# A message-passing kernel whose row gathers wait on the vector engine: the waits of the first 18 groups are taken out, and the distance cutoff becomes one activation

## The chip, the cores and the metric

The kernel runs on one core of a Trainium2 chip. The metric is the time of one execution in device microseconds (us). A core has several engines that run side by side and wait for each other through semaphores: TensorE (PE; its weight loads are listed as PEld), VectorE (DVE), ScalarE (ACT), GpSimd (POOL) and SyncE (SP). SP, ACT and POOL also issue DMA transfers; a name with q behind it (SPq, ACTq, POOLq) is the queue of such an engine.

## The reference, cut to what matters

There are N = 12500 nodes with 64 features (`x`) and E = 200000 edges with 64 features; the edges are sorted by their destination `dst`.

```python
nodes = x[[src, dst]].reshape(E, 128)
gates = ssp(edge_attr @ We1 + be1) @ We2 + be2
soft_cutoff = 1.0 - sigmoid(5.0 * (edge_weight1 - (CUTOFF - 1.5)))    # CUTOFF = 5
h = ssp(nodes @ Wn1 + bn1) @ Wn2 + bn2
message_sum = zeros.at[dst].add(h * gates * soft_cutoff)
new = x + ssp(message_sum @ Ws1 + bs1) @ Ws2 + bs2
out = layernorm(x + new)                     # ssp(v) = softplus(v) - log(2)
```

## The kernel before, in words

**Groups.** The edges are cut into 391 groups of 512; a group is four columns of 128 edges, one edge to a partition. The source rows `x[src]` of a group come by four gathers on POOL's queue (`gather`, line 230): an indirect DMA takes 128 row numbers from `src_i` and puts 128 rows of 64 floats into the tile `xg`. POOL does nothing else but these gathers; there are 1523 of them. In 40 places from group 28 on a column's 128 rows are instead copied row by row by plain DMAs of SP and ACT (`fetch`, line 250); the padding at the end needs none.

**Buffers.** `xg` has AHEAD + BEHIND = 14 + 4 = 18 buffers. Groups 0 to 17 find a fresh one; group g from 18 on waits for the matmul that reads group g - 18's buffer last (`scatter`, line 371).

**Before the loop.** SP loads `src_i`, the destinations, the transposed `x` (in seven parts, line 493), the distances (`cut`) and more. From these the kernel works out the offsets of each half group's window of destinations, and it makes a table of x @ Wn1's lower half in memory: seven parts of two halves (lines 576 to 586), each half by matmuls (L581), two copies out of PSUM, one by ACT (L583) and one by DVE (L584), a store (L585) and a DVE memset that clears the space for the sums (L586). In the third part (`i == 2`, lines 598 to 606) the cutoff is worked out in place in `cut`: DVE's `tensor_scalar` (L599), ACT's sigmoid (L600), which needs a table load before it and one behind it (L601), and DVE's second `tensor_scalar` (L602). DVE goes on with the cast of `rel` (L603) and two subtractions (L606).

**When a gather may start.** Groups 0 to 4 (FREE = 5) wait only for `src_i`. Groups 5 to 13 stand in `waiting`: they are handed out over the halves of the table (lines 587 and 588). Groups 14 to 17 are asked for in steps 0 to 3 of the loop (line 641, `i < BEHIND`). For both, `gather(g, after=True)` first has DVE write one column of the new tile (line 223), so POOL's gather waits until DVE has come to that instruction in its own order.

**The loop.** Step i (lines 632 and on) is an order written out by hand. SP loads for group i + 5, POOL gets group i + 14's gathers, PE runs layer 1 of group i + 1, layer 2 of the group before it and `scatter` of group i - 3; PE also transposes group i + 3 (L299), which is where a gather's data is first read. All of a step's waits are put on its first matmul, `layer1_bias` (L309): it waits for loads of group i + 1 and for the gathers of group i + 3. From step 380 on the distances are shorter. 25 blocks of nodes are finished in between as soon as their edges are complete. The tail behind the last group takes the last block.

Of the kernel before, what the change touches and what calls it, by code (L numbers as in the profile page):

```python
# [42 lines left out]
F32 = mybir.dt.float32  # L43
# [3 lines left out]
AF = mybir.ActivationFunctionType  # L47
OP = mybir.AluOpType
# [9 lines left out]
P = 128  # L58
# [8 lines left out]
AHEAD = 14  # L67
# [1 line left out]
SPREADS = 5  # L69
CATCH_UP = 10  # L70
PREPARE = 5
FREE = 5
BEHIND = 4


# [4 lines left out]
CUTOFF = 5.0  # L80
# [41 lines left out]
def gnn_resnorm_kernel(ctx: ExitStack, tc: tile.TileContext, a: dict, out: bass.AP, E: int):  # L122
    nc = tc.nc
# [42 lines left out]
    packed, at = {}, 0  # L166
# [48 lines left out]
    def padding(g, k):  # L215
        return g * GE + k % 2 * HE + k // 2 * P >= E

    def gather(g, after=False):

        xg = loads.tile([P, K, P], F32, name="xg", bufs=AHEAD + BEHIND)  # L220
        xgs[g] = xg
        if after:
            nc.vector.memset(xg[:, 0, :1], 0.0)
        for k in range(K):
            if (g, k) in by_rows:
                continue
            if padding(g, k):
                nc.vector.memset(xg[:, k, :D], 0.0)
                continue
            note(("gather", g), nc.gpsimd.indirect_dma_start(  # L230
                out=xg[:, k, :D], out_offset=None, in_=x,
                in_offset=bass.IndirectOffsetOnAxis(ap=src_i[:, g, k : k + 1], axis=0)))
# [124 lines left out]
    def layer2(g):  # L357
        layer2_edge(g)
        layer2_node(g)
# [118 lines left out]
    with tc.manual_schedule():  # L478
# [4 lines left out]
        with tc.tile_pool(name="prep", bufs=1) as prep:  # L483
# [3 lines left out]
            PARTS = 7  # L487
# [10 lines left out]
            dist = cut.rearrange("p g k -> p (g k)")  # L498
# [1 line left out]
            dst_i = rel.bitcast(I32)  # L500
            nc.sync.dma_start(dst_i.rearrange("p g k -> p (g k)"), a["dst_l"])

            waiting = {}
            for g in range(AHEAD):
                if g < FREE:
                    gather(g)
                else:
                    waiting.setdefault(min(5 * (g - FREE) // 3, 2 * PARTS - 1), []).append(g)

            nc.vector.memset(one, 1.0)  # L510
            nc.vector.memset(half, 0.5)
# [1 line left out]
            nc.vector.memset(ones3, 1.0)  # L513
            nln2 = prep.tile([P, 1], F32, name="nln2")
            nc.vector.memset(nln2, -LN2)
            brow = prep.tile([1, 4, D], F32, name="brow")
            nc.scalar.dma_start(brow.rearrange("o i d -> o (i d)"), a["biases"])
            nc.scalar.dma_start(consts[:, FIRST:], a["consts"][:, FIRST:])
# [57 lines left out]
            for i in range(PARTS):  # L576
                for c in range(i * CP, (i + 1) * CP, CP // 2):
                    m = CP // 2
                    ps = z_tile().rearrange("p b (k f) -> p (b k) f", k=K)
                    for k in range(m):  # L580
                        nc.tensor.matmul(ps[:, k, :], xT[:, c + k, :], wnb, start=True, stop=True)  # L581
                    tb = prep.tile([P, m, 2 * D], F32, name="tb", bufs=6)
                    nc.scalar.copy(tb[:, :K, :], ps[:, :K, :])  # L583
                    nc.vector.tensor_copy(tb[:, K:, :], ps[:, K:m, :])  # L584
                    nc.sync.dma_start(by_node[:, c : c + m], tb)  # L585
                    nc.vector.memset(sums[:, c * P : WIDE if c + m == NCH else (c + m) * P], 0.0)  # L586
                    for g in waiting.get(c // m, []):
                        gather(g, after=True)
                if i == 1:
                    nc.vector.tensor_copy(base_i[:1], base_b[:1])  # L590
                    nc.vector.tensor_scalar(base_i[32:33], base_b[32:33], float(8 * D), None, OP.mult)
                    nc.vector.tensor_scalar(rows_i, rows_i, float(4 * D), None, OP.mult)
                    for k in range(2):
                        nc.vector.tensor_copy(be3[:, k, :], rows[:, 0, :])
                    for k in range(K):
                        nc.vector.tensor_copy(row3[:, :, k, :], rows[:, 1:3, :])
                        nc.vector.tensor_copy(rs3[:, k, :], rows[:, 3, :])
                if i == 2:
                    nc.vector.tensor_scalar(dist, dist, CUTOFF - 1.5, 5.0, OP.subtract, OP.mult)  # L599
                    nc.scalar.activation(dist, dist, AF.Sigmoid)  # L600
                    nc.scalar.preload_act_table_set("natural_log_exp_and_others")  # L601
                    nc.vector.tensor_scalar(dist, dist, -1.0, 1.0, OP.mult, OP.add)  # L602
                    nc.vector.tensor_copy(rel, dst_i)  # L603
                    for t in range(2):
                        r = rel[:, :, 2 * t : 2 * t + 2]
                        nc.vector.tensor_sub(r, r, base_b[:, :NH].rearrange("p (g h) -> p g h", h=2))  # L606


        with tc.tile_pool(name="finish", bufs=1) as finish:
# [16 lines left out]
            def at(f, g, *more):  # L626
                if 0 <= g < NG:
                    f(g, *more)
# [5 lines left out]
            for i in range(-3, last - 1):  # L634
                now = parts.pop(i, [])
                early = [part for part in now if part.tensor]
                at(load, i + LOADS)
                fetch(i, 0, 0)
                fetch(i, 0, 1)
                if i >= 0:  # L640
                    at(gather, i + AHEAD, i < BEHIND)
                if i < ends:
                    needs = [("xcopy", i + 1), ("load", i + 1)]
                    needs += [(name, g) for g in ahead[i] for name in ("gather", "onehot")]
                    if i >= -1:
                        layer1_bias(i + 1, *needs)
                    for g in second[i]:
                        layer2_edge(g)
                    if i >= -1:
                        layer1_edge(i + 1)  # L650
                        for part in early:
                            part.tensor(tx_tile())
                    if i >= -1:
                        layer1_node(i + 1)
                    for n, g in enumerate(third[i]):
                        scatter(g, zs[i + 1][:, 1, HE + 2 * W * n : HE + 2 * W * (n + 1)])
                    at(exps, i + 1)
                    fetch(i, 1, 0, 0, ROWS // 2)
                    at(logs, i + 1)
                    fetch(i, 1, 0, ROWS // 2, ROWS // 2)  # L660
                    for g in ahead[i]:
                        transposes(g)
                        xcopy(g)
                    fetch(i, 1, 1)
                    for g in second[i]:
                        layer2_node(g)
                    for g in second[i]:
                        hcut(g)
                        message(g)
                    for g in third[i]:  # L670
                        window(g)
                    for part in early:
                        part.others()
                    at(softplus, i + 1)
                else:
                    for g in ahead[i]:
                        transposes(g)
                        xcopy(g)
                    layer1_bias(i + 1)
                    layer1_edge(i + 1)  # L680
                    for part in early:
                        part.tensor(zs[i + 1][:, 1, HE:])
                    layer1_node(i + 1)
                    exps(i + 1)
                    logs(i + 1)
                    for g in second[i]:
                        layer2(g)
                        hcut(g)
                        message(g)
                    softplus(i + 1)  # L690
                    for g in third[i]:
                        scatter(g, tx_tile()[:, : 2 * W])
                        window(g)
                    for part in early:
                        part.others()
                for g in ahead[i]:
                    at(onehot, g + 2)
                for part in now:
                    if not part.tensor:
                        part.others()  # L700
                complete = third[i][-1] + 1 if third[i] else 0
                if blocks and complete >= blocks[0][1] - PREPARE and not begun:
                    begun = node_block(*blocks[0][0], finish)
                    begun.pop(0).others()
                if blocks and complete >= blocks[0][1]:
                    steps = next(steps for steps in BLOCK_STEPS if i + steps[-1] < last - 1)
                    for n, part in zip(steps, begun):
                        parts.setdefault(i + n, []).append(part)
                    rest = begun[len(steps) :]
                    blocks.pop(0)  # L710
                    begun = None
# [12 lines left out]
            square, variance, root, scale, store = (part.others for part in rest)  # L724
# [31 lines left out]
    with tc.If(far > 0), tc.tile_pool(name="outside", bufs=1) as o:  # L756
# [7 lines left out]
        with tc.For_i(0, NG, 1) as g:  # L764
# [13 lines left out]
            xg = o.tile([P, K, 2, D], F32, name="xg2")  # L778
# [120 lines left out]
```

## Time and profile before

| | us |
|---|---|
| three runs, lowest / median / highest | 1963.82 / 1969.16 / 1975.15 |
| the profiled execution, own time | 1968.45 |
| its span in the trace | 1966.5 |
| PE busy in the span | 1750.5 (89%) |
| POOL busy | 1445.0 (73%) |
| DVE busy | 1077.2 (55%) |
| ACT busy | 922.5 (47%) |
| first gather starts / last gather starts | 3.2 / 1919.7 |
| first matmul of layer 1 (L309) | 78.2 |

The busy time of an engine leaves out register moves, semaphore instructions and the issue of DMAs. A line of the timeline has a start, a duration, the engine, the line of the kernel, the operation, what it writes and reads, and in square brackets the idle time just before it with what ended it. In the table of stretches each engine has its busy time and, in parentheses, the number of its instructions.

### The profile page before, as it was taken

Reading aid. Unit: us, or ns where it says so; the run is one execution under the profiler, and the core shown is the slowest. Engines: PE = TensorE matmul, PEld = TensorE weight load, DVE = VectorE, ACT = ScalarE, POOL = GpSimd, SP = SyncE. Lnnn points to the kernel's source line nnn. Section 1 sums busy time; section 2 is a strip of 40 time slices with the busy share of each in tenths; the row PEclk is TensorE's granted clock in tenths of the full one; section 3 lists DMA queues with packets and bytes.
Section 4 is the critical chain, followed back from the end, with each engine's and each line's share of the span. In section 5 each row is a group of like instructions: output and inputs, shape, how many; then the busy total and the mean of one; then the engine's idle time right before and its main releaser. Section 6 shows DMA issues by size and latency. Waiting matters only on the chain.

```text
span 1966.5 us, 46634 instructions
## 1 busy us (share of the span) xinstructions
PE 1750.5 (89%) x11373; PEld 1491.4 (76%) x11373; DVE 1077.2 (55%) x2774; ACT 922.5 (47%) x1318; POOL 1445.0 (73%) x1527
## 2 busy tenths in 40 slices
PE   5899999999998988889889988998989989998896
PEld 4777877877777777777777777777777777777775
DVE  4455555555555555555555555555555555555654
ACT  1344545555454444445444444444544454444443
POOL 6777777777777777777777777777777777777770
PEclk9999999999999999999999999999999999999997
DMA  8422222222222222222222222222222222222220
GB/s 242 128 70 65 70 64 72 65 72 65 73 67 73 65 73 67 67 66 69 65 69 66 67 70 67 69 67 70 68 70 73 64 74 68 70 72 71 69 61 13
DMA packets 149240, 143.45 MB, mean 73 GB/s; under 512 B 50073, under 2 KB 96621, under 8 KB 148964
## 3 DMA queue, kind: packets, MB, share of 16 engines
q1 hardware_dynamic: 92972, 88.12, 15.6%
q0 software_dynamic: 48736, 50.00, 11.3%
q10 hardware_dynamic: 7256, 2.27, 0.6%
q8 instruction: 97, 1.59, 0.3%
q14 instruction: 179, 1.47, 0.3%
HBM read 130.59 MB, written 9.63 MB: 71 GB/s over the span
## 4 chain that ended last, share of the span: by engine, by line
PE 46%; ACTq 14%; DMA 10%; SPq 10%; issue 9%; ACT 5%; DVE 3%; POOL 3%; DVEq 0%; POOLq 0%
ACTq L250 11%; PE z L320 10%; PE gh L348 7%; PE gh L354 6%; PE z L314 5%; PE z L371 5%; DMA xg<-in_x,src_i 4%; PE tx L299 4%; DMA wns<-table 4%; SPq L250 4%; ACT u L331 3%; ACTq L244 3%; PE z L309 3%; POOL xg L230 3%; PE gh L345 2%
## 5 line engine op out<-in xcount | busy, mean ns | idle before, releaser
L230 POOL DMA_INDIRECT xg<-in_x,src_i x1523 | 1444.8, 949 | 475.3 <-issue 319.4
L331 ACT ACTIVATE u<-z 128x768 f32<-128x768 f32 x392 | 315.9, 806 | 624.4 <-PE z L371 316.7
L334 ACT ACTIVATE u<-u,one 128x768 f32<-128x768 f32 x392 | 366.0, 934 | 238.5 <-ACT u L331 236.7
L339 DVE SCALAR_TENSOR_TENSOR s<-u,z 128x768 f32<-128x768 f32 x392 | 372.6, 950 | 171.2 <-ACT u L334 154.6
L363 DVE TENSOR_TENSOR h<-gh,cut 128x256 f32<-128x256 f32 x391 | 165.2, 423 | 478.3 <-PE gh L354 472.0
L320 PE MATMUL z<-xT,wns 106*128 106x256 f32 x1564 | 423.9, 395 | 0.0
L354 PE MATMUL gh<-consts,s 128*128 128x64 f32 x3128 | 395.7, 270 | 0.0
L354 PEld LDWEIGHTS gh<-consts,s 128*128 128x128 f32 x3128 | 384.7, 194 | 0.0
L320 PEld LDWEIGHTS z<-xT,wns 106*128 106x128 f32 x1564 | 307.4, 198 | 45.8 <-ACT xT L304 0.7
L348 PEld LDWEIGHTS gh<-consts,s 128*128 128x128 f32 x1564 | 206.7, 192 | 122.8 <-issue 122.3
L348 PE MATMUL gh<-consts,s 128*128 128x128 f32 x1564 | 282.4, 304 | 0.0
L371 PEld LDWEIGHTS z<-xg,msg 128*128 128x128 f32 x1512 | 237.9, 199 | 22.9
L309 PE MATMUL z<-ones,be 3*128 3x256 bf16 x391 | 105.3, 269 | 167.8 <-DMA wns<-table 64.9
L299 PE MATMUL tx<-consts,xg 128*106 128x128 f32 x1524 | 240.8, 280 | 4.0 <-DVE xg L285 2.7
L388 DVE TENSOR_TENSOR sums<-sums,z 64x42 f32 x756 | 148.7, 197 | 171.4 <-ACT u L331 75.2
L314 PE MATMUL z<-eT,consts 128*128 128x256 f32 x782 | 242.4, 393 | 0.0
L304 ACT COPY xT<-tx 106x512 f32<-106x512 f32 x391 | 221.6, 567 | 15.5 <-PE tx L299 15.3
L371 PE MATMUL z<-xg,msg 128*128 128x84 f32 x1512 | 223.3, 271 | 0.0
L309 PEld LDWEIGHTS <-be 3*128 3x128 bf16 x391 | 35.4, 91 | 206.6 <-issue 102.9
L299 PEld LDWEIGHTS tx<-consts,xg 128*106 128x106 f32 x1524 | 181.8, 144 | 5.1 <-DVE xg L285 3.0
L367 DVE TENSOR_TENSOR msg<-gh,h 128x256 f32<-128x256 f32 x391 | 165.9, 424 | 13.4
L345 PE MATMUL gh<-row,ones 3*128 3x512 bf16 x391 | 145.9, 373 | 0.0
(103 smaller groups left out, 714.0 us busy)
## 6 DMA issues: line engine op xcount, KB each, us to landing
eT<-in_eT SPq DMA_DIRECT2D x195, 256.0 KB
xr<-in_x ACTq DMA_DIRECT2D x2944, 0.2 KB
xr<-in_x SPq DMA_DIRECT2D x2176, 0.2 KB
xg<-in_x,src_i POOLq DMA_INDIRECT x1523
wns<-table SPq DMA_DIRECT2D x782, 21.0 KB
table<-tb SPq DMA_DIRECT2D x14, 448.0 KB
sums<-in_xT SPq DMA_DIRECT2D x7, 455.0 KB
y<-in_x SPq DMA_DIRECT2D x24, 128.0 KB
```

The source lines that it names most:

```text
L230: note(("gather", g), nc.gpsimd.indirect_dma_start(out=xg[:, k, :D], out_offset=None, in_=x, in_offset=bass.IndirectOffsetOnAxis(ap=src_i[ ...
L250: ins = queues[queue].dma_start(row_tiles[n, "in"][r + j : r + j + 1, :D].bitcast(U8), x_bytes[:, bass.ds(row_at[queue][j], 4 * D)])
L299: nc.tensor.transpose(tx[:, k, :], xgs[g][:, k, :DW], ident)
L304: note(("xcopy", g), nc.scalar.copy(xT, xTs[g]))
L314: nc.tensor.matmul(zs[g][:, 0, :HE], we1.rearrange("a h d -> a (h d)"), eTs[g], start=False, stop=True, skip_group_check=True)
L320: nc.tensor.matmul(zn, wns[:, g % REST, h, :], xTs[g][:, h], start=True, stop=True, skip_group_check=True)
L331: nc.scalar.activation(us[g][:, part], z_of(g)[:, part], AF.Exp)
L334: nc.scalar.activation(us[g][:, part], us[g][:, part], AF.Ln, bias=one)
L339: nc.vector.scalar_tensor_tensor(ss[g].rearrange("p i t e -> p (i t e)")[:, part], us[g][:, part], BIG, z_of(g)[:, part], OP.min, OP.max)
L348: nc.tensor.matmul(v[:, 0, t], ss[g][:, 0, t, :], we2, start=False, stop=False, skip_group_check=True)
L354: nc.tensor.matmul(ghs[g][:, 1, 2 * t + h, :], ss[g][:, 1 + h, t, :], wn2, start=False, stop=h == 1 and t == 1, skip_group_check=True)
L371: ins = nc.tensor.matmul(sc, msgs[g][:, 2 * t : 2 * t + 2, :].rearrange("p h f -> p (h f)"), xgs[g][:, 2 * t : 2 * t + 2, D:DW], start=t = ...
```

## The change

It takes the parameter `after` out of `gather`, with its memset on DVE, and the lists `waiting` and `FREE`. All 14 groups that are issued before the loop are issued at one place ahead of the table, and groups 14 to 17 in steps 0 to 3 as before; none of them writes to its tile on DVE first. The cutoff 1 - sigmoid(5 (d - 3.5)) is computed as sigmoid(-5 d + 17.5), with the scale as a number and the bias in a new column `steep`; the two `tensor_scalar` operations on DVE go.

```diff
-FREE = 5
...
-    def gather(g, after=False):
+    def gather(g):
         xg = loads.tile([P, K, P], F32, name="xg", bufs=AHEAD + BEHIND)
         xgs[g] = xg
-        if after:
-            nc.vector.memset(xg[:, 0, :1], 0.0)
...
-            waiting = {}
             for g in range(AHEAD):
-                if g < FREE:
-                    gather(g)
-                else:
-                    waiting.setdefault(min(5 * (g - FREE) // 3, 2 * PARTS - 1), []).append(g)
+                gather(g)
...
+            steep = prep.tile([P, 1], F32, name="steep")
+            nc.vector.memset(steep, 5.0 * (CUTOFF - 1.5))
...
-                    for g in waiting.get(c // m, []):
-                        gather(g, after=True)
...
                 if i == 2:
-                    nc.vector.tensor_scalar(dist, dist, CUTOFF - 1.5, 5.0, OP.subtract, OP.mult)
-                    nc.scalar.activation(dist, dist, AF.Sigmoid)
+                    nc.scalar.activation(dist, dist, AF.Sigmoid, bias=steep, scale=-5.0)
                     nc.scalar.preload_act_table_set("natural_log_exp_and_others")
-                    nc.vector.tensor_scalar(dist, dist, -1.0, 1.0, OP.mult, OP.add)
...
                 if i >= 0:
-                    at(gather, i + AHEAD, i < BEHIND)
+                    at(gather, i + AHEAD)
```

## The prediction

> **What bounds the kernel now.** I read the list of costliest groups first. PE is the busiest engine, but POOL's line catches the eye:
>
> ```profile
> L230 POOL DMA_INDIRECT xg<-in_x,src_i x1523 | 1444.8, 949 | 475.3 <-issue 319.4
> ```
>
> Busy plus idle is 1444.8 + 475.3 = 1920 us: POOL issues gathers from start to end, and the idle time is the same 0.30 us before each. The table of stretches shows whether it ever pauses (POOL is the fifth engine):
>
> ```profile
> 100.00:484.00 384.00, 357.00 (x2425) 305.63 (x2423) 209.18 (x539) 192.89 (x264) 290.33 (x308) 1.00 0.27 68
> 484.00:1885.00 1401.00, 1261.48 (x8259) 1075.55 (x8259) 780.56 (x2008) 673.41 (x969) 1059.68 (x1120) 0.97 0.27 69
> ```
>
> 384 / 308 = 1.247 and 1401 / 1120 = 1.251 us per gather, in the free early part and in the late one alike. So POOL is a clock that ticks every 1.249 us (0.944 + 0.305) and waits for no buffer. Is PE tied to it? The early steps take about 4.35 us on PE, four gathers take 5.0 us, so the 11 groups of lead that the gathers have at 85 us are used up: by the counts of instructions up to 480 us, 92 steps have begun and only one gather is to spare. From there they go together. Up to 1497 us the trace has 301 first matmuls and 1185 gathers; the next step needs groups up to 303, which are 304 x 4 - 31 columns taken by rows = 1185 gathers: exactly the last one issued. At fourteen sampled times from 600 to 1850 us the last gather needed lies within 3 of the last one issued. The waits at L309 name other transfers too (`wns`, 64.9 us); but at 1497 us SP has issued 614 of them, 307 groups, six ahead of need, so the gather in the same wait explains them better. The last touch is late:
>
> ```profile
> 1857.03 0.94 POOL L230 DMA_INDIRECT xg<-in_x,src_i  x1 [0.30 <-DVE l_s L422]
> ...
> 1859.54 0.26 PE L309 MATMUL z<-ones,be 3*128 3x256 bf16 x1 [0.61 <-DMA xg<-in_x,src_i]
> ```
>
> The matmul starts 2.5 us after the gather that it needs. Behind this PE runs on its own to the end, 107 us. So the time is the gathers' stream up to here plus a constant, and **whatever moves the stream moves the end.** Where does POOL lose time? Its own timeline has two holes:
>
> ```profile
> 27.83 0.94 POOL L230 DMA_INDIRECT xg<-in_x,src_i  x1 [0.30 <-issue]
> 33.07 0.94 POOL L230 DMA_INDIRECT xg<-in_x,src_i  x1 [4.30 <-DVE xg L223]
> ...
> 79.19 0.94 POOL L230 DMA_INDIRECT xg<-in_x,src_i  x1 [0.30 <-issue]
> 84.75 0.94 POOL L230 DMA_INDIRECT xg<-in_x,src_i  x1 [4.61 <-DVE xg L223]
> ```
>
> Both end with DVE's memset: group 5 waits for the table's first half, group 14 for step 0.
>
> **The change part by part.** *The holes.* Start to start they are 5.24 and 5.56 us instead of 1.249: 3.99 + 4.31 = 8.3 us. With no wait on DVE both go. The other 11 memsets of this kind held nothing: POOL came to them later than DVE.
>
> *What is late next.* Group 18 is the first to need a used buffer, that of group 0. POOL would reach it at 3.21 + 72 x 1.249 + 2.3 (stretches, below) = 95.4 us. Group 0's scatter in the old trace:
>
> ```profile
> 94.83 0.57 PE L371 MATMUL z<-xg,msg 128*128 128x84 f32 x4
> ```
>
> It ends at 95.40, so even an unmoved start of the loop costs POOL about 0.1 us. Later groups are no danger: scatters follow every 4.35 us, gathers every 5.0.
>
> *The stretches.* Some gathers take longer beside certain DVE operations:
>
> ```profile
> 45.82 1.58 POOL L230 DMA_INDIRECT xg<-in_x,src_i  x1 [0.30 <-issue]
> 46.31 0.97 DVE L599 TENSOR_SCALAR cut<-cut 128x1564 f32<-128x1564 f32 x1
> ...
> 47.31 1.51 ACT L600 ACTIVATE cut<-cut 128x1564 f32<-128x1564 f32 x1 [1.16 <-DVE cut L599]
> ...
> 48.83 1.28 ACT L601 ACT_TABLE_LOAD   x1
> 48.85 0.97 DVE L602 TENSOR_SCALAR cut<-cut 128x1564 f32<-128x1564 f32 x1 [1.57 <-ACT cut L600]
> 48.95 1.88 POOL L230 DMA_INDIRECT xg<-in_x,src_i  x1 [0.30 <-issue]
> 49.74 0.97 DVE L603 CAST rel<-rel 128x1564 f32<-128x1564 int32 x1
> ```
>
> Against 0.944 us the gather at 45.82 loses 0.63 beside L599, that at 48.95 loses 0.93 beside L602 and L603, and one at 51.13 (1.40 us) loses 0.45 beside L606: 2.0 in all. L599 and L602 go. L603 and L606 stay and now follow each other without a pause; by these rows they cost between 0 and 2.0, and I take the middle of L603's 0 to 0.97, 0.5, and L606's 0.45. Saved: 2.0 - 0.95 = 1.0 us, bounds 0 and 2.0. The other stretches before group 18 (0.55 beside the cast L523, 0.27 beside L590, some of 0.1) stay; with the 0.95 they are the 2.3 used above. The Trainium skill, "SBUF — State Buffer", section "Who interferes with whom", says that copy, cast and tensor_scalar can take the port pair that DVE shares with GpSimd and then block it for the whole instruction, while tensor_tensor is not seen to stall descriptor generation. The row beside L606, a tensor_tensor, speaks against the second half. By the page alone only the cast would remain, and the estimate would be 0.4 us more saved.
>
> *The cutoff.* In the old trace ACT waits 1.16 us for L599 and its two table copies for DVE's chain; the table's PE work stands still until 53.12. Without the pair the sigmoid can start when its table is loaded, 46.15, and ends at 47.66; the second load (1.28) lets ACT copy at 48.96, not 50.13. DVE does L603 and L606 from 46.4 to 49.2 and can copy at 49.6, not 52.52. The table and the loop start 2.9 us earlier. Scale and bias on the activation: the nearest rows are Exp without a bias column (0.806 us) and Ln with one (0.934), so at most 0.13 us more; the new memset is 0.06 us in DVE's wait for `dst_h` (8.64 us). Both are hidden. The 2.9 us are worth **nothing at the end**, since PE has 11 groups of lead to use up before it meets the gathers; they only keep group 18's wait at zero. If PE were the bound, they would be the whole gain.
>
> *The transfers brought forward.* 52 gathers (groups 5 to 17) start up to 9 us earlier, in a stretch where the DMA engines are 65% to 87% busy. Their queue took 11.3% of 1966.5 us for 1523 gathers, 0.146 us of all engines each. At most 9.3 / 1.249 = 7 more gathers lie in the stretch ahead of the loop: 1.1 us, below the 2.9 saved; nothing on SP or ACT is moved. The Trainium skill, "DMA: Bandwidth & Descriptors", section "Issuing engines are not separate DMA queues", speaks against the change: DMAs of all engines interleave on the same 16 engines, so a gather issued early takes its turn from the table's stores. By the estimate of the row above, this leaves the sum as it is; the page gives no price for it.
>
> **Sum.** 8.3 + 1.0 = 9.3 us off the stream, and off the profiled execution's 1968.45: **1959.2 us**. The trace's span would be 1957.2. The median of the runs lies 0.7 above the profiled execution; against it 1959.2 is 0.51% faster, against its own time 0.47%. Can PE follow? It must win 9.3 us between its first meeting with the gathers at 480 us and the last at 1859. Its waits at L309 that name a gather sum to 21.2 us, with those that name `wns` 86 us. It can.
>
> **The rivals.**
> - *PE, not POOL, becomes the bound.* If the `wns` waits are real, SP paces many steps. For: SP's queue is nearly without pause in the middle. Against: it waits for PE's scatters 5 to 9 us in every 100 us there, so it has room. If PE gets only the earlier start of 2.9 us and some of the 21.2 us, the gain is 3 to 6 us: 1962.5 to 1965.5.
> - *The gathers still wait.* Group 5 or 14 could be held by something that the memset hid, a buffer or the second part of `src_i`. Against: all 18 buffers are fresh, and that load was issued at 1.22 us, ahead of `dst_h`, which was there at 9.85. Then only the stretches are gained: 1967.5.
> - *Slower: crowded DMA delays the table, and group 18's wait eats the gain.* Until 29 us, where gathers run without a gap, two small dependent transfers took 8.05 (`low_d`) and 6.77 us (`base_b`); around 75 us, behind fewer gathers, the table's last store took 2.81 and the first `wns` 1.89. If five dependent transfers ahead of the loop (a part of `x`, two of the eight halves that reuse a buffer of `tb` and so wait for an earlier store, the last store, `wns`) each rise by 5.5 us, scatter(0) comes 27.5 - 2.9 = 24.6 us later and POOL stands still as long: 24.6 - 9.3 = 15.3 us slower, 1983.8. It decides from a loop start that is 9.3 us later than now; from 19 us later the loss passes 0.5%. Against it: 1.1 us of engine time, as above.
>
> **Chances.** Forecast 0.70 (bounds 1958.2 to 1960.2; the three runs before differ by 0.3% either way, so a median may fall 4 us to a side); PE bound 0.14; gathers still wait 0.08; slower 0.08. The range leaves out the slow case and a little below: from 1958.2 less 0.3%, 1952, to 1970. Faster by over 0.5%, about what a measurement of this kernel can tell from no change, means below 1959.3: the forecast lies on the line, and two thirds of it, 0.47, I put below, since the stretches could save a little more. Within 0.5%: the rest of the forecast, the PE bound and the waiting gathers, 0.23 + 0.14 + 0.08 = 0.45. Slower: 0.08.
>
> **What the new profile would show.** No gap before a gather over 0.3 us up to group 18 (the 73rd gather, near 95 us); the last gather near 1910.4 instead of 1919.7; L309 first near 75.3; scatter(0) near 92.5. The pieces of the chain near 1850 still meet gathers. I am wrong if the last gather is early but the end is not (PE bound), or if POOL has a hole near 95 us that ends with L371 (slow case).

## The result and the profile after

The changed kernel took **1963.05 us** in the median of 20 runs (1958.56 to 1968.99), the kernel before, in 20 runs beside it, 1969.88 (1962.87 to 1979.13): ratio 0.9964 with a 95% interval of 0.9952 to 0.9976, some 7 us. A second measurement (run f1_whole below) gave 0.9956 [0.9938, 0.9975]. The profiled execution took 1965.5 us, its span is 1963.7. Forecast was 1959.2, 9.3 us less than the 1968.45 before.

The page of the kernel after, the costliest group of POOL (busy time, mean ns of one, idle time before):

```profile
L227 POOL DMA_INDIRECT xg<-in_x,src_i x1523 | 1448.3, 951 | 467.2 <-issue 335.9
```

POOL's idle time fell by 8.1 us (475.3 to 467.2), nearly the 8.3 of the two holes. But its busy time rose by 3.5 us (1444.8 to 1448.3) for the same 1523 gathers: some of them now take longer. The timeline of POOL, after, where the holes were (start, length, and in brackets the idle time ahead):

```profile
29.29 0.94 POOL L227 DMA_INDIRECT xg<-in_x,src_i  x1 [0.30 <-issue]
...
77.90 0.94 POOL L227 DMA_INDIRECT xg<-in_x,src_i  x1 [0.31 <-issue]
...
98.11 0.94 POOL L227 DMA_INDIRECT xg<-in_x,src_i  x1 [0.30 <-issue]
...
1915.04 0.95 POOL L227 DMA_INDIRECT xg<-in_x,src_i  x1 [0.30 <-issue]
```

The gather at 77.90 is the first of group 14, which came at 84.75 before; that at 98.11 is the first of group 18, the first to need a used buffer, and it has no wait. It was due near 95 by the forecast. The last gather starts at 1915.04, not at 1910.4 as forecast, and not at 1919.68 as before. Scatter(0), on PE after, comes early enough (94.83 before):

```profile
91.25 0.57 PE L368 MATMUL z<-xg,msg 128*128 128x84 f32 x4
```

A part of what is missing is seen around the cutoff, after:

```profile
45.08 2.28 POOL L227 DMA_INDIRECT xg<-in_x,src_i  x1 [0.30 <-issue]
45.50 1.60 ACT L592 ACTIVATE cut<-cut,steep 128x1564 f32<-128x1564 f32 x1
45.64 0.91 DVE L594 CAST rel<-rel 128x1564 f32<-128x1564 int32 x1
46.58 1.86 DVE L597 TENSOR_TENSOR rel<-rel,base_b 128x782 f32<-128x782 f32 x2
...
47.67 1.59 POOL L227 DMA_INDIRECT xg<-in_x,src_i  x1 [0.31 <-issue]
```

DVE's `tensor_scalar` pair is gone and the sigmoid takes 1.60 us with scale and bias (1.51 before). But the two gathers beside the cast and the subtractions lose 1.34 + 0.65 = 2.0 us against 0.944, where the forecast left 0.95.

Each stream of gathers can be split up to group 18 (its first gather) into what POOL waited and what single gathers took over 0.944 us, with the same sum for the loop behind:

```
us                       waits to 18   stretches to 18   group 18 at   stretches behind   last gather
before                       8.33            3.40           104.86           3.72            1919.68
after                       -0.02            4.90            98.11           5.72            1915.04
f1_whole (again)            -0.02            4.73            97.85           4.01            1913.11
f2 (cutoff alone)            5.86            2.10           101.09           3.96            1916.18
f3 (14 to 17 wait)           2.96            4.79           100.98           3.86            1916.03
```

So up to group 18 the change takes 8.3 us of waits off and puts 1.3 to 1.5 us of stretches on: 6.8 to 7.0 us net. The loop's own stretches differ by 1.7 us between two profiles of one kernel (5.72 and 4.01).

### The profile page after: what moved, and what is told of

Same layout as the page of the kernel before. It is cut to its first block, busy times and chain, and to the rows that moved or that the text cites. A ratio compares the mean times of both kernels' runs of the same rounds, so it can differ in the third digit from the quotient of the medians.

```text
span 1963.7 us, 46608 instructions
## 1 busy us (share of the span) xinstructions
PE 1760.8 (90%) x11373; PEld 1498.9 (76%) x11373; DVE 1075.8 (55%) x2760; ACT 923.3 (47%) x1318; POOL 1448.5 (74%) x1527
## 4 chain that ended last, share of the span: by engine, by line
PE 50%; ACTq 15%; issue 9%; DMA 8%; SPq 7%; ACT 5%; DVE 3%; POOL 2%; DVEq 0%; POOLq 0%
ACTq L247 12%; PE z L317 11%; PE gh L345 8%; PE gh L351 7%; PE z L311 5%; PE z L368 5%; PE tx L296 4%; ACTq L241 3%; ACT u L328 3%; DMA xg<-in_x,src_i 3%; PE z L306 3%; DMA wns<-table 3%; SPq L247 3%; PE gh L342 3%; POOL xg L227 2%
## 5 line engine op out<-in xcount | busy, mean ns | idle before, releaser
L227 POOL DMA_INDIRECT xg<-in_x,src_i x1523 | 1448.3, 951 | 467.2 <-issue 335.9
L306 PE MATMUL z<-ones,be 3*128 3x256 bf16 x391 | 105.8, 271 | 156.0 <-DMA wns<-table 53.6
L301 ACT COPY xT<-tx 106x512 f32<-106x512 f32 x391 | 221.5, 567 | 15.6 <-PE tx L296 15.3
```

Of the source, the lines that this page charges most:

```text
L227: note(("gather", g), nc.gpsimd.indirect_dma_start(out=xg[:, k, :D], out_offset=None, in_=x, in_offset=bass.IndirectOffsetOnAxis(ap=src_i[ ...
L301: note(("xcopy", g), nc.scalar.copy(xT, xTs[g]))
```

## The experiments

T1 in the expectations is the prediction's theory, that POOL's stream of gathers sets the end. T2 says that PE's own work does, so that the holes cost nothing. T3 is the slower rival: gathers without a pause hold the table up, and group 18's wait hands that on; after the first four runs it got the form that the later expectations give.

**Two kinds of chip.** The first result and the runs f1 to f4 come from chips on which the kernel before takes 1970 to 1973 us. The runs e1 to e4 and g1 to g4 fell on two other chips, on which the same kernel before takes 2507 and 2468 us. Each run's ratio is to the kernel before on its own chip. The kernel before has no profile from a late chip (as the second kind is called below); e2, which keeps all waits, stands in for it. What sets the two kinds apart in the traces is how long after the modelled end of a matmul the increment of its semaphore is recorded (1304 matmuls carry one):

```
us late             median    90%    99%    longest
before               0.01    0.01   0.84      3.6
after                0.01    0.02   0.45      3.3
f1_whole             0.01    0.02   0.45      6.4
e2_cutoff_only       2.34    5.23   6.65     10.7
e1_gathers_free      2.12    4.86   5.77     34.6
g3_gathers_free      2.34    5.04   5.79     56.2
```

I call them **prompt** and **late** chips. A matmul's end is modelled, so it could also be the matmul that ends late; the engine that waits for it sees the same.

### e1 and g3: the waits alone

The whole change, but with the old cutoff (two operations of DVE around a plain sigmoid); g3 is the same kernel as e1.

```diff
-                    nc.scalar.activation(dist, dist, AF.Sigmoid, bias=steep, scale=-5.0)
+                    nc.vector.tensor_scalar(dist, dist, CUTOFF - 1.5, 5.0, OP.subtract, OP.mult)
+                    nc.scalar.activation(dist, dist, AF.Sigmoid)
...
+                    nc.vector.tensor_scalar(dist, dist, -1.0, 1.0, OP.mult, OP.add)
```

> The gathers' part of the change alone: no wait on DVE, the cutoff as it was (two tensor_scalar on DVE and the sigmoid). If the gathers' stream sets the end: the holes of 8.3 us go, the stretches beside DVE's operations stay or grow, so 5 to 8 us less than before, nearly all of the whole change's 7. If PE sets the end: no more than 3 us less. If the whole change's gain comes from the cutoff: no gain here.

> Only the waits of the gathers go; the cutoff keeps DVE's two operations. The same kernel gave 1.015 on the chip with late increments. T1: the holes go and the two operations go on stretching gathers (1.5 to 2 us), so ratio 0.997 where increments come at once: within 2 us of the whole change. T2 (the cutoff's earlier loop start of 3 us is the gain): 1.000. On a chip with late increments T3 says 1.015 again.

Measured, both on late chips: e1 2546.47 us, ratio **1.0153** [1.0126, 1.018]; g3 2505.78, ratio **1.0161** [1.0133, 1.0189]. There the change's main part makes the kernel slower by 39 and 38 us. POOL's timeline of e1 shows the wait that takes the place of the holes:

```profile
93.00 0.94 POOL L227 DMA_INDIRECT xg<-in_x,src_i  x1 [0.30 <-issue]
160.38 0.94 POOL L227 DMA_INDIRECT xg<-in_x,src_i  x1 [66.44 <-PE z L368]
```

POOL does groups 0 to 17 without a pause, the last at 93.0, and then stands 66 us until scatter(0), because the loop began at 143.0 us. Why, ACT's timeline of e1 tells; L576 is ACT's copy of a half of the table out of PSUM:

```profile
50.60 0.59 ACT L576 COPY tb<-z 128x512 f32<-128x512 f32 x1 [19.72 <-remote]
89.80 0.58 ACT L576 COPY tb<-z 128x512 f32<-128x512 f32 x1 [38.62 <-remote]
104.55 1.07 ACT L576 COPY tb<-z 128x512 f32<-128x512 f32 x2 [14.16 <-remote]
```

and PE's of the same stretch, the matmuls for the first two of these copies:

```profile
31.52 3.36 PE L574 MATMUL z<-consts,sums 65*128 65x128 f32 x14 [7.67 <-issue]
51.83 3.36 PE L574 MATMUL z<-consts,sums 65*128 65x128 f32 x14 [16.95 <-issue]
```

These copies wait for PE alone (no buffer of `tb` is used again yet). PE's matmuls for the three end at 34.88, 55.19 and 94.39; the increments are recorded at 50.58, 89.78 and 104.52, that is 15.7, 34.6 and 10.1 us late. "remote" is how the trace names a releaser that it cannot place. In between ACT, DVE and PE do nothing and SP stores nothing; only the gathers go on, and up to 42 us transfers that were issued earlier. From 60 to 90 us the DMA engines are 12% to 13% busy, so it is not crowded transfers that hold the table. The third increment is late after POOL's last gather has ended at 93.94, so the delay outlasts the gathers; then the table goes on at its usual pace.

### e2 and f2: the cutoff alone

```diff
-                    nc.vector.tensor_scalar(dist, dist, CUTOFF - 1.5, 5.0, OP.subtract, OP.mult)
-                    nc.scalar.activation(dist, dist, AF.Sigmoid)
+                    nc.scalar.activation(dist, dist, AF.Sigmoid, bias=steep, scale=-5.0)
...
-                    nc.vector.tensor_scalar(dist, dist, -1.0, 1.0, OP.mult, OP.add)
```

> The cutoff's part alone: one sigmoid with scale and bias, the gathers wait on DVE as before. If the gathers' stream sets the end: the second hole, which ends with step 0's memset, gets about 3 us shorter since the loop starts 3 us earlier, the first hole stays: about 3 us less than before, the loop's first matmul near 75. If PE sets the end: the same 3 us, from the earlier start. If the cutoff is worth nothing at the end: 0.

> One sigmoid, and only the gathers of groups 14 to 17 wait for nothing of DVE; those of groups 5 to 13 keep their waits. T1: the second hole (4.31 us) goes, the first (3.99) stays, so about half of the whole change: ratio 0.998, the first gather of group 5 near 33, that of group 14 near 80 us. T3, on a chip with late increments: the waits of groups 5 to 13 hold POOL back whenever the table is late, so that no standstill of the table over 8 us is left before step 0, and the ratio is 1.000 and not 1.015. T2: 0.999 to 1.000 on either.

The edit of f2 missed its aim. It took the wait from groups 14 and up where the lists of the table's halves hand gathers out, but groups 14 to 17 are asked for in the steps of the loop, so all waits stayed and f2 is the same program as e2. It is read as that: **the cutoff alone**, on a late chip 2509.68 us, ratio 1.0003 [0.9979, 1.0026], and on a prompt one 1966.11, ratio 0.9984 [0.9966, 1.0003]. POOL's holes in f2:

```profile
32.61 0.94 POOL L230 DMA_INDIRECT xg<-in_x,src_i  x1 [3.96 <-DVE xg L223]
...
81.12 0.94 POOL L230 DMA_INDIRECT xg<-in_x,src_i  x1 [2.53 <-DVE xg L223]
```

The loop starts at 74.6 instead of 78.2, DVE comes to group 14's memset sooner, and the second hole shrinks from 4.61 to 2.53 us of idle time; the stretches fall by 1.3. Together group 18 comes 3.8 us earlier, and the last gather 3.5. With the waits kept, the cutoff alone is worth about 3.5 us of the stream on a prompt chip; in time the ratio's interval still includes no change. On the late chip the waits of e2 hold POOL back whenever the table is late: no copy of the table waits over 7.2 us, and the loop starts at 86.9 (e1: 143.0).

### e3 and e4: more gathers, fewer gathers

e3 adds 16 gathers into a spare tile behind group 4's; e4 leaves out the first gather of every tenth group from group 21 on, 37 in all.

```diff
+                if g == 5:
+                    for j in range(16):
+                        nc.gpsimd.indirect_dma_start(out=spare[:, j, :], out_offset=None, in_=x, ...)
                 gather(g)
```

```diff
+            if k == 0 and g >= 18 and g % 10 == 1:
+                continue
```

> The changed kernel with 16 more gathers, into a tile that nobody reads, put ahead of group 5's. They hold POOL for 16 x 1.249 = 20.0 us at a time when the gathers are 11 groups ahead of PE; PE's own work is unchanged. If the gathers' stream sets the end: 15 to 20 us slower than the changed kernel, some 1978 to 1983. If PE's own pace sets it: 0 to 5 us slower.

> The changed kernel with one of the four gathers left out in every tenth group from 21 on, 37 of 1523 (those 128 edges use old rows, so the sums differ). The stream is 37 x 1.249 = 46 us shorter. If the gathers' stream sets the end and PE has room to follow: 35 to 46 us faster than the changed kernel, some 1917 to 1928. If PE's own pace is close behind: 5 to 20 us faster, and the trace shows the gathers running ahead until they wait for buffers.

Measured on the late chip: e3 2569.53 us, ratio 1.0252 [1.0218, 1.0286]; e4 2509.33, ratio 0.9998 [0.9974, 1.0022]. In e4, g2 and g4, whose gathers up to group 18 are those of the whole change, the loop starts at 139.6, 138.9 and 139.7; in e3 at 160.4, later by the 20 us that its 16 gathers take: the table stands still for as long as the gathers last. Against e1, which has the old cutoff (its loop starts at 143.0), e3 takes 23 us more and e4 37 us less. So a gather has a price of about 1 us there as well. But it can't be POOL's stream that sets this price: in the loop POOL waits some 480 us for PE in e1 as in e4, all along. So the 35 to 46 us expected came true in size without the reason given for them, and why a gather costs that much on a late chip stays open.

### f1: the whole change again, beside its parts

> The whole change, unaltered, beside its parts. T1 (POOL's stream of gathers sets the end; the holes are the gain): ratio 0.996 where PE's semaphore increments are recorded within 0.02 us of the matmul's end, as in the first profiles of before and after (median 0.01 us). T3 (PE's increments come late, median 2.1 to 2.3 us, and gathers without a pause make some in the prologue 10 to 35 us late): on a chip with such late increments 1.015, as with the waits alone taken away. T2 (PE's own work sets the end): 0.998 to 1.000 on the first kind of chip, 1.000 on the second.

On a prompt chip 1963.34 us against 1973.01, ratio **0.9956** [0.9938, 0.9975]. As T1 said. Not run on a late chip.

### f3: groups 5 to 13 free, 14 to 17 still wait

```diff
-                if g < FREE:
+                if g < 14:
                     gather(g)
```

together with the new cutoff.

> One sigmoid, and groups 5 to 13 wait for nothing; groups 14 to 17 keep their wait. T1: the first hole goes, but groups 5 to 13 are then done by 75 us, and POOL waits for the memset of group 14 from there: the table's end at 74 sets it, so the second hole shrinks or stays near 4; ratio 0.998. T3, on a chip with late increments: the 36 gathers of groups 5 to 13 run without a pause from 28 to 73 us and the table stands still beside them for 30 us or more; ratio 1.008 to 1.015. T2: 0.999 to 1.000 on either.

Prompt chip: 1966.59 us, ratio 0.9966 [0.9951, 0.9981]. POOL's timeline in f3, without the first hole and with the second:

```profile
30.51 0.94 POOL L230 DMA_INDIRECT xg<-in_x,src_i  x1 [0.30 <-issue]
...
81.01 0.94 POOL L230 DMA_INDIRECT xg<-in_x,src_i  x1 [3.27 <-DVE xg L223]
```

POOL comes to group 14 at 78 and waits for step 0 as before. To remove the first hole alone moves group 18 by 0.1 us against f2 (100.98 and 101.09): the time won there is waited away at group 14. Only the whole change brings 97.85. In time f2, f3 and f1 stand at 0.9984, 0.9966 and 0.9956; their order is that of T1, but the intervals overlap, and the first measurement of the whole change (0.9964) is no faster than f3. So it is the stream in the traces that tells the parts from one another, not the time.

### f4: 186 gathers fewer

As e4, in every second group (`g % 2 == 1`).

> The whole change without the first gather of every second group from group 19 on: 186 of 1523 gathers fewer, 232 us of POOL's stream at 1.249 us each (so the sums differ from the reference's). T1: the end falls until PE's own work stops it, between 14 us (all that PE waits for gathers by the profile of after) and 68 us (with its waits for wns) below the whole change: ratio to before 0.96 to 0.99. T2: within 5 us of the whole change. T3, on a chip with late increments, where POOL waits for PE: within 5 us of the whole change there.

Prompt chip: **1864.01 us**, ratio 0.9448 [0.942, 0.9476], 99 us under the whole change. T1's 14 to 68 us fell short. T2 is out: no work of PE was taken away, its 11373 matmuls are all there. The page of f4 and, behind it, two of its waits:

```profile
PE 1719.2 (92%) x11373; PEld 1463.2 (79%) x11373; DVE 1064.3 (57%) x2760; ACT 922.1 (49%) x1318; POOL 1271.2 (68%) x1341
```

```profile
POOL xg L229 <- PE z L370: 106.5, 112, 4.1
...
PE z L308 <- DMA wns<-table: 7.5, 6, 2.2
```

The same waits of the kernel after (us in total, times, longest):

```profile
PE z L306 <- DMA wns<-table: 53.6, 56, 2.4
...
PE z L306 <- DMA xg<-in_x,src_i: 14.1, 15, 1.2
```

With fewer gathers the waits named after `wns` fall from 53.6 to 7.5 us and those named after `xg` from 14.1 to 0.2, although SP loads `wns` as before. They were the gathers' all along, as the prediction read them; in after, 52 of the 56 waits named after `wns` end 27 us or more after SP has issued the load, while the first, at 74 us, ends 1.9 us after the issue. And now POOL waits for PE, some 5 us in every 100 from 200 us on: 1864 us is the pace of PE and what works with it. Of the 99.9 us between the spans of after and f4, PE's busy time is 41.6 (1760.8 to 1719.2) and its idle time 58.3 (202.9 to 144.6); against f1, on the same chip, 25.2 and 69.9 of 95.0. The expected 14 to 68 us counted waits alone, and the idle time is of that size; the busy time was not foreseen (see the end).

### g1: which operations of DVE stretch a gather

Idle work on scratch tiles behind the subtractions: 5 tensor_tensor, 6 copies, 6 tensor_scalar, 6 memsets, 5 scalar_tensor_tensor, and 5 copies on ACT.

> The whole change with idle work on scratch tiles (128x1024 f32) behind the subtraction that makes rel, while POOL gathers without a pause: 2 memsets, then 5 tensor_tensor with two SBUF inputs, 6 copies, 6 tensor_scalar, 6 memsets, 5 scalar_tensor_tensor with two SBUF inputs on DVE, and 5 copies on ACT. It is read by the length of each gather (0.944 us alone); the table comes some 30 us late, so the time says nothing. Theory A, which the prediction leant on (an operation of DVE of any kind can stretch a gather, a tensor_tensor by up to 0.45): the gathers beside each kind are 1.2 to 1.9 us. Theory B (only copy, cast and tensor_scalar, as the notes have it): 0.95 beside tensor_tensor, scalar_tensor_tensor and ACT, longer beside the rest. Theory C (two SBUF inputs, and casts between types; not plain f32 copies, tensor_scalar or memsets): 1.5 or more beside tensor_tensor and scalar_tensor_tensor, 0.95 beside the others.

It answered nothing: on a late chip the table stood still, and DVE came to this work from 116 to 145 us, while POOL stood idle for 100.6 us up to its gather at 194.26.

What can be said comes from the six profiles of prompt chips (before, after, f1 to f4): a least-squares fit of each gather's length over 0.944 us to the us that it lies beside each kind of DVE operation. Operations that always come together can't be told apart and are left out.

```
us lost per us beside it   gathers   operation on DVE
 0.92                           6    cast, int32 to f32 (rel, 128x1564)
 0.53                           6    cast of dst_h
 0.53                          12    tensor_tensor, both inputs in SBUF (rel, base_b)
 0.27                         147    tensor_tensor, both inputs in SBUF (y, rstd)
 0.05                        2308    tensor_tensor, both inputs in SBUF (consts, rel), 0.33 us each (one-hot)
 0.02                          96    memset (sums, 128x896)
 0.00                        2488    tensor_tensor, one input in PSUM (gh, cut)
-0.01                        3291    scalar_tensor_tensor, one input in PSUM (u, z)
 0.00                          95    copy out of PSUM (tb)
```

None of the three theories fits. A is out, since operations that read PSUM cost a gather nothing; B, since the subtractions cost it 0.53; C, since the one-hot has both inputs in SBUF and costs 0.05, and since beside L599 alone, a tensor_scalar, the gather at 45.82 of before lost 0.63. The first three rows rest on six to twelve gathers.

### g2: a gather that SP takes over

f4 says that each gather fewer on POOL is worth time as long as PE can follow. g2 lets SP fetch two pieces of four rows in each step, not one and a half: 6 gathers fewer, 768 row transfers more.

```diff
-    return max(0, 2 * i + 2 if queue else (3 * i + 4) // 2)
+    return max(0, 2 * i + 2)
```

> The whole change, and SP fetches two pieces of rows in each step instead of one and a half: 6 gathers of 1523 fewer on POOL, 768 rows more on SP. T1: 6 x 1.249 = 7.5 us less than the whole change, ratio to before near 0.992, unless SP falls behind (by the profile of after a piece takes SP about 2.0 us with its register loads, so two of them, wns and eT fill 4.9 to 5.0 of a step's 4.9 us); then 0.995 to 1.01, with waits for xr or wns in its profile. T2: 0.996, like the whole change.

On a late chip: 2828.83 us, ratio **1.1455** [1.1438, 1.1471], 323 us above g3, 0.42 us for each row added. A step now takes 7.0 us (g3: 6.0), and the eight rows alone took SP 4.83 us at 1000.06 and 4.40 at 1006.51. What SP waits for PE's scatters (us in total, times, longest) tells how much room its queue has. In the kernel after, on a prompt chip:

```profile
SPq L275 <- PE z L368: 79.7, 59, 5.1
SPq L267 <- PE z L368: 51.8, 35, 5.2
```

In g3 and in g2:

```profile
SPq L267 <- PE z L368: 15.4, 4, 8.2
...
SPq L275 <- PE z L368: 10.3, 4, 4.7
```

```profile
SPq L267 <- PE z L368: 15.2, 7, 7.2
...
SPq L275 <- PE z L368: 6.9, 5, 5.8
```

131.5 us on the prompt chip, 25.7 and 22.1 on the late one: there SP has little room even in g3, and g2 loads just this queue. Part of the reason may lie in SP's own instructions. A register move of SP, as ahead of each row, takes 0.029 us in the median; none of 2960 takes over 0.2 in before, after or f1, but 539 in e1, 482 in g3 and 457 of 3728 in g2. From one row to the next within a piece of four it is 0.34 us in the mean on prompt chips, 0.52 to 0.58 on late ones. What g2 does on a prompt chip stays open.

### g4: a standstill of PE

60 matmuls without use in step 150, 25.7 us of PE.

```diff
+                    if i == 150:
+                        idle = tx_tile()
+                        for _ in range(60):
+                            nc.tensor.matmul(idle[:, :256], ident, consts[:, :256], start=True, stop=True)
```

> The whole change, and in step 150 PE does 60 matmuls (128x128 by 128x256, f32) whose result is not used: some 20 to 25 us in which it does nothing else. T1: POOL gathers on behind them into the free buffers, PE is then 16 to 20 gathers late and makes it up before the end, since without 186 gathers it took 100 us less: within 4 us of the whole change, spare gathers near 18 after the step and back to 0 before step 300. T2: 20 to 25 us slower, ratio to before 1.007 to 1.009.

On a late chip: 2515.25 us, ratio 1.0181 [1.0162, 1.02]. Against g3, which has the old cutoff, that is 9.5 us more, between the 4 of T1 and the 20 of T2, and the intervals of the two ratios overlap. It decides nothing for the prompt chip, where the theories differ; f4 does.

## Why the prediction was right, and where it was off

**What bounds the kernel: right.** The end hangs on POOL's stream. f4 shows it by taking gathers away alone (99 us), and with it the reading that waits named after `wns` were the gathers'. PE had room for far more than the 9.3 us asked of it: 58 to 70 us of idle time went in f4, somewhat less than the 86 us of waits that the prediction counted, and the rest came by a higher clock. The time alone would not have told: the rival in which PE becomes the bound was priced at 1962.5 to 1965.5, and both the profiled execution (1965.5) and the median (1963.05) lie in it. The last gather and f4 speak for POOL's stream.

**The holes: right in size.** 8.33 us of waits are gone in both profiles of the whole change, 8.3 were forecast, and no other wait took their place on a prompt chip. f3 adds that the two are not independent: while the second is kept, taking the first away moves group 18 by 0.1 us.

**Group 18: right.** No wait; scatter(0) ended at 91.8, the gather came at 98.1.

**The stretches: this step failed.** It counted 1.0 us saved, bounds 0 and 2.0. Measured up to group 18: 1.3 to 1.5 us lost, outside the bounds. The sum of 9.3 becomes 6.8 to 7.0 by this term alone. Two things were missed. The stretch around the cutoff cost the gathers 2.0 us before and costs 2.0 after, not 0.95: the cast and the subtractions, which stand in one piece now, take what the pair of `tensor_scalar` took. And it held that "the other stretches before group 18 stay". Without the holes the gathers meet DVE's operations at other moments. After, two gathers of POOL, each with an operation of DVE that begins in the course of it:

```profile
39.28 1.76 POOL L227 DMA_INDIRECT xg<-in_x,src_i  x1 [0.30 <-issue]
39.66 0.55 DVE L583 CAST base_i<-base_b 1x896 int32<-1x896 f32 x1
...
69.53 1.82 POOL L227 DMA_INDIRECT xg<-in_x,src_i  x1 [0.30 <-issue]
...
70.27 0.99 DVE L282 TENSOR_TENSOR xg<-consts,rel 128x168 f32<-128x168 f32 x4
```

Before, the longest gathers beside the same two operations, which had begun ahead of the gather:

```profile
40.55 1.21 POOL L230 DMA_INDIRECT xg<-in_x,src_i  x1 [0.30 <-issue]
...
74.06 1.08 POOL L230 DMA_INDIRECT xg<-in_x,src_i  x1 [0.30 <-issue]
```

Together that is 0.55 + 0.74 us more, nearly the whole of the loss. So the price of one and the same operation hangs on how it meets a gather; that the order of the two starts decides it isn't shown. The Trainium skill, "SBUF — State Buffer", section "Who interferes with whom", which the prediction weighed, says that tensor_tensor was not seen to stall descriptor generation, though it also has two SBUF inputs contend with what GpSimd reads. The first does not hold here: 0.53 us lost per us beside the subtractions. The second fits them and the 0.00 beside a tensor_tensor that reads PSUM, but not the 0.05 beside the one-hot. The measured numbers decide.

**The cutoff: worth nothing at the end, not tested as it was meant.** With the waits kept it is worth about 3.5 us of the stream on a prompt chip (f2), since an earlier loop shortens the second hole, a way that the prediction didn't name. With the waits gone that way is closed. The waits alone were not run on a prompt chip. The loop's start was forecast for 75.3 and came at 74.4, so on that chip the transfers brought forward did not delay the table.

**The end.** In the first pair of profiles the last gather moved 4.6 us and the span 2.8; in f1 they moved 6.6 and 7.6. Both measured gains, 6.8 and 9.7 us by the medians, are of the order of the stream's 7. What follows the last gather is not the constant that the prediction took it for: from its start to the end it is 46.8 us before, 48.6 after, 45.8 in f1, 47.9 in f2 and 53.1 in f3, whose profiled execution is slower than that of before although its last gather comes 3.7 us earlier. That the time came out inside the range says little by itself: 1952 to 1970 also holds the kernel before. And the chances leaned the wrong way: the largest, 0.47, was put on a gain over 0.5%, and measured were 0.36 and 0.44%.

**The slower rival: it exists.** It was given 0.08 and a price of 15.3 us, with crowded transfers as its cause. On late chips its place (table late, POOL waits at group 18) is just what happens, by 38 to 39 us; the loop of e1 starts 56 us later than that of e2, and the threshold was 9.3. The cause is another: it is not the transfers that hold the table up but PE's increments, which come late where gathers run without a pause. That gathers without a pause bring it about is shown by seven kernels without the waits that all stand still (POOL waits 64 to 101 us at group 18), one with them that does not, and e3, where 16 gathers lengthen it by 20 us. By what path is not shown, nor what makes a chip late. Within the trace of before, nothing pointed to it.

## What to carry to other kernels

When a stream of one engine sets the end, count its waits and its stretched instructions in one ledger up to a common point: once a wait is gone, the stream meets other operations at other moments, and their price must be taken anew. Waits ahead of DMAs can cost some tenths of a per cent on one chip and be worth 1.5% on the next, so before they go, measure on more than one. Here the cutoff alone was not slower on either kind of chip (0.9984 and 1.0003); the whole change is the best on prompt chips, and its main part is a loss on late ones.

## What the chip showed that was not expected

- PE seems to pay for a wait twice, by the idle time and by the clock behind it. The granted clock is 0.984 to 0.99 in the four runs of f4, 0.964 to 0.976 in the twelve of f1, and the same matmuls take 41.6 us less in f4 than in after. In the table of stretches of the kernel after and of f4 (PEclk is the third number from the end):

```profile
484.00:1885.00 1401.00, 1270.88 (x8286) 1082.12 (x8286) 784.76 (x2017) 675.76 (x972) 1060.01 (x1118) 0.96 0.29 69
```

```profile
484.00:1760.00 1276.00, 1205.02 (x8131) 1026.21 (x8130) 757.79 (x1975) 662.99 (x956) 910.92 (x962) 1.00 0.27 71
```

  PE is busy 91% of the stretch in the first and 94% in the second. It isn't the number of gathers as such: the prediction's row of before for 100 to 484 us, where they are just as dense and PE does not yet wait for them, has 1.00. In the trace the clock falls to 0.50 for 3.4 us or a few times that, as here in before, where PE had just waited 1.47 us up to 521.02:

```profile
518.00:522.00 4.00, 2.53 (x22) 2.11 (x22) 2.48 (x6) 1.82 (x4) 3.09 (x4) 1.00 0.40 106
522.50:525.50 3.00, 3.00 (x12) 2.65 (x11) 1.20 (x2) 0.87 (x3) 2.13 (x3) 0.50 0.15 37
```

  Between 150 and 1880 us there are 28 such falls in before, 26 in after and 4 in f4. In the 4 us ahead of each PE was idle for 22% to 59%, against 6% in the median of all such stretches. That the wait brings the fall about is read from this order, not tested.
- Two chips run the kernel before 25% and 27% slower (2468 and 2507 us, granted clock 0.84 to 0.87) than the others, with increments of PE recorded 2.1 to 2.3 us late in the median against 0.01 in the runs of the table above. In g2, on one of these chips and the slowest of all, the median is only some 0.3 us from a matmul's end to the next recorded increment, so the lateness isn't fixed for a chip.
- On these two chips SP's shortest instructions are held up too (g2 above), and fewer increments of DMA semaphores are in the trace: 900 to 917 of the first gather semaphore in e2 and e1, 2985 to 2993 in before, after and f1. Every run lists a granted clock, so every run was recorded; whether the chip is slow or its recording was not separated.
